# Transposing a quarter of the softmax weights by DMA in two 16-bit planes, in a decoder layer on one core

## The chip, the cores and the metric

The kernel runs on one core of one Trainium2 chip. The metric is the time of one execution on the device, in microseconds (us).

## The reference

One pre-norm decoder layer on x of shape (8, 112, 512): causal self-attention with rotary positions, cross-attention to a latent context of shape (8, 375, 128), and a gated feed-forward net in fp8. Heads: 16 of width 32.

```python
# self-attention                                     # x = x + attn(layernorm(x))
q = rope(x @ Wq + bq); k = rope(x @ Wk + bk); v = x @ Wv + bv
scores = einsum('bshd,bthd->bhst', q, k) / sqrt(32)  # causal mask
out = einsum('bhst,bthd->bshd', softmax(scores), v) @ Wo + bo
# cross-attention                                    # x = x + xattn(layernorm(x), ctx)
qp = q @ Wq.T; k, v = split(latent_kv @ Wkv_expand.T, 2)
attn = softmax(where(tril, qh @ kh.T / sqrt(32), min))  # mask: key <= query
out = (attn @ vh) @ Wout.T
# feed-forward                                       # x = x + ffn(layernorm(x))
act = gelu(qdot(x, w_gating[0])) * qdot(x, w_gating[1]); out = qdot(act, w_linear)
```

Because of the mask only the first 112 context positions take part. `qdot` casts both operands to fp8 (e4m3).

## The kernel before

**Staging.** x is held in SBUF as seven tiles of 128 tokens. Layer norm, projections and output projections go by these tiles or by column ranges; attention goes by batch (8 batches of 112 tokens). Float32 projections are done as three matmuls on a high and a low part (`mm3`, line 363; `split_evac`, lines 324 and 325, makes the two parts of an activation, `split_weight`, lines 281 and 283, those of a weight). The FFN is fp8 (lines 572 and 597).

**Attention of one batch** (`attention`, called for "a", self, and "x", cross). One step of TensorE makes the scores of all 16 heads into four banks (line 420). They form four groups of four heads, c = 0 to 3. For each group VectorE adds the mask and takes the row minimum (line 429), ScalarE takes the exponential with its row sum (line 432), VectorE the reciprocal (435), GpSimd or VectorE normalises the 112 x 448 weights P (436). TensorE transposes the group's four 112 x 112 blocks into the PSUM tile pspt (443), ScalarE or VectorE copies that to pts (`copy`, line 320). When all four groups are there, one step of 32 matmuls multiplies them by the values (AV, line 453), and its result is split into fm (`split_evac`).

**Other users of what the change touches.** `flip` (lines 332 to 335) is the DMA transpose that the kernel has already: the normalised input of the FFN, 128 x 512 in bf16 (xw), is transposed into xt on SP's queue and cast to fp8. GpSimd also does half of the weight splits (283), part of the rotary additions (402), the power of layer norm (307), the bias additions (500), and issues three casting loads of 1 MB for the FFN's weights (509, 512). SP's queue issues every other DMA: the weights' staging loads (256), the rotary row swaps (400), the values' stores (478), the outputs (605).

**Order.** All steps are put in a list when the kernel is built, and `ORDER`, a long string of step numbers, says in which order they are issued; a letter behind a number chooses the engine (a ScalarE, d VectorE, p GpSimd) where a step allows two. Each engine runs its own steps in that order and waits for the data. `CAPS` gives the number of buffers of each kind (t: temporaries of 512 floats a row, with pts, ws for weight staging and others as limits inside it); a buffer is given to the next user in the order when its last user is listed.

Of the kernel before, what the change touches and what calls it, by code (L numbers as in the profile page):

```python
# [10 lines left out]
BF = mybir.dt.bfloat16  # L11
F8 = mybir.dt.float8e4
# [19 lines left out]
PAIR = 4  # L32

# [17 lines left out]
class Plan:  # L51
# [47 lines left out]
    "p": 8, "s": 4, "t": 15, "w": 4, "w8": 1, "sm": 12, "m": 4, "pt": 1, "av": 1, "ws": 4, "pts": 7, "fg": 6, "fo":  # L99
    2, "rp": 5, "xn": 3, "f": 5, "cx": 3, "P": 4, "a8": 1, "nw": 20, "warm": 1, "vt": 2,  # L100
}
ORDER = """
1 23-24 37 40 25-26 43 46 85-87 94 22 88 0 89 95-98 2-20 90-91 21 38 103 112 39p 99 41 42p 92 100-101 44 113 104 102
114 105 45d 106 93 107 257-258 272-273 259 274 47 275-276 32 28 49 115 29 311 116 48p 277 260 278 108 50 261 279-282
262 109 263 283 320 51d 312 264-267 55 35 52 36 56 117 110 287 53 73 58 284 111 57d 64 118-119 288-290 268 120 59 54d
321 60d 74 75p 65 27 61 286 269 66d 302 322 62 63d 313 303-304 323 305 67 33 76 30 70-71 68 72p 155 291 156-157
121-122 158 123 159 292 124-129 160 130 161-163 131 189 132 190 164 191 165 293 192 294 193-194 324 134 133 1128 544
34 31 271 285 136 166-167 170 135 195 295 168 69d 196 296 197 297 138-139 198 140 199 141-142 298 200 143 172 202 299
201 144 173 145 174 146-147 175 148 545 77 169 1129 546p 314-315 306 223 176-177 149 178-180 224 240 225 547 82 325
137p 78d 151 150 153 83 316 307 171p 152 204 270 241 181-183 185 184 242 326 226-227 243 228 530 327-328 154d 528-529  # L110
203 187 186 244 229 206 230 245 231-232 246 548 233 207 247 234 248-249 236 235 250 308 208 309 209-210 317 211 318
212-215 310 188d 205p 329 216 251-253 330-333 217 334-335 219 319 218 237-238 254 79 255 220-221 336 465-469 337 470
346-347 338 348-349 339 350-352 340 353 471-472 354 473 355 474 356-357 256d 239d 341-342 222d 380 475 397 476 398 359
80 565 477 84d 358 360 592 361 343 549p 1130p 527 362p 81p 300 363-366 399 580 578 478-479 594 582 608 584 606 566 570
596 367-369 602 604 568 572 590 593 609 567 381 510 382 511 370-371 512 383 372 513-516 373-374 569 573 571 574
375-376 517-521 400 384 401 385 402 607 597 605 579 583 603 522 575d 585 581 591 595 617 576 414 386 586 587p 577a 523
377 301 344 524 378 415 387-388 588 416 403 389 610 618 598 620 622 599d 624 630 611d 634 623 589a 417 390-391 418 600
419 404 420 405-406 421 407 392 636 601d 621 635 619 625 612 422-423 408 424-425 631 626 642 632 393 646 654 637 633
643 613a 658 660 638 648 647 649 659 409-410 345p 627p 379p 639p 431 448 432 628 629a 655 614 394-395 644-645 427 426
650 656 412 428 411 429 640 449 433-434 450 435 615 531 651p 641d 657 661 690 616 721 662 693 663p 652 695 697 691 727  # L120
653a 698 480 436-438 481 439 664 482 451-454 483 455-457 440 458 441-442 484-485 459 731 729 719 709 715 733 707 703
692 665d 696 694 705 699 710 728 722 720 708 732 706 704 525 413p 700d 717-718 701 702a 716 666 763 430p 443-444 711
712p 460 667 723 462-463 550 446 445 668 724p 396p 713 730 734 714a 768 461 735 766 769 486 1139-1141 1142a 788 767
1135 725 726a 736p 1136-1137 1143 487-488 1144-1145 792 764 794 770-771 765 778 776 780 790 1138d 772 489 737 495 490
496 491 497 464p 773p 447p 779 777 738a 804 782 795 800 802 806 783 781 492 793 789 791 784 807 803 801 805 774 739
836 775d 1146d 796 853 855 851 785p 786 797p 841 787d 837 808 498 669 499-500 670 501 798 740 854 852 856 842 849
843-844 838 879 799d 877 875 839-840 880 850 526 809p 671 502 672 503-504 673-675 810 676 505 677 506 678-679 845 873
865 861 811a 846p 867 857 863 741 876 864 874 868 866 878 862 858p 847 909 812 507 848d 912 493-494 508-509 553 556
532 859 916 869 914 928 881 922 870p 917 913 860a 742-743 680 744 926 745 871 746-747 681 910 813 915 927 551 936-937
923 911 872d 934 940 814 924 682 882p 918 748-751 883 752 815 753 816-826 884a 935 925 929 533 754 946-947 941 950 930  # L130
755-756 952 938 554 948 683 827-828 919p 534p 931p 920 885 951 939 921a 886 982 932 942 829 684 887 949 953 557 985
983 830 987 933d 552p 943p 831 888-893 944 894-897 559 986 984 988-989 954 955p 990 945a 1011 1009 997 1007 991 1001
999 956 1012 685 992p 555p 1131-1133 898-899 995 998 1002 1000 996 957d 1021 1013 1025 1019 1003 1023 993 958 900 994d
1055 1004p 1005 1010 1014 1022 1008 959 1026 1024 1020 1006a 1134a 558p 541 538 535 961-967 1015 901 1016p 1070 902
1060 1056 1027 1068 1058 960 1072 1062 1057 1059 1063 1061 1017 757 1080 1018d 968-972 1028p 1029 560 1069 1086 686
1064 1094 1084 1074 1030a 1071 1151-1152 687 1031 973 1065p 1087 1073 1075 1032 1066 832 1096 1082 903 1098 1076 1081
1097 1083 1099 1085 1095 1092-1093 1067d 1033 542 688 1147 1153 1154d 1034-1038 1077p 1078 1039-1040 1088 758 904
1079d 1089p 1100 1148 833 1149 1041-1042 1090 1150d 689 1043-1044 1159 1045 536 1091a 1101p 974 905 975 759 834-835
1046 1102 1103a 1160-1161 906 1104 760 1155-1157 539 1105 1162d 761 1158a 1163 1107-1111 1106 537d 762 1047-1048 543d
907-908 540d 1164 1198 1112-1114 1211 1115 1199 1116 1212 1200 1117 1201-1203 1118 1165p 1119-1122 976 564 977-978  # L140
561d 1049-1050 1224 1204 1225 1205 1213 1226 1214-1215 1227 1216 1206 1228 1207-1208 1217 1209 1229-1230 1237-1238
1231 1218-1222 1232 1239-1246 1233 1247 1234 1248 1235 1223d 1210d 1123-1124 1249d 1051 1236a 979-981 1125 1350 1126
1379 1363 1357 1355 1052 1367 1369 1365 1351 1353 1393 1389 1387 1391 1377 1275 1250 1276 1251 1277 1252 1278-1279
1253 1280-1281 1254 1282-1283 1255-1256 1284 1257-1259 1285-1288 1260 1289-1293 1261 1294-1295 1380 1358 1053 1356
1354 1352 1054 1359 1360d 1364 1366 1390 1378 1370 1361 1262 1296 1263 1297 1381 1375 1127 1368 1371 1372d 1402 1362a
1388 1376 1382 1392 1394 1373 1407 1374a 1403 1408 1300 1264-1265 1301 1298 1383 1417 1405 1395 1384p 1266 1302 1267
1303-1304 1268 1305 1385 1306 1269 1409 1299d 1421 1431 1386d 1429 1415 1406 1404 1418 1410-1411 1396p 562 1412p
1325-1326 1270 1307 1327-1328 1271 1308 1272 1397 1309 1273 1310-1312 1329 1422 1430 1416 1398a 1419 1441 1274d 1427
1443 1420 1432 1423 1433 1444-1445 1434 1439-1440 1446 1428 1313 1330 1314 1331 1315-1316 1413 1399-1400 1442 1424p
1414d 1475 1425 1332-1337 1435 1482 1436p 1426a 1338 1317 1339 1437 1340 1318 1341-1343 1319 1344 1483 1492 1494 1476  # L150
1493 1478-1479 1495 1480 1447 1490 1401 1438d 1502 1504 1481 1477 1484 1506 1491 1448p 1345 1320 1346-1347 1449 1170
1321 1171 1348 1172 1516 1166 1322-1323 1167-1168 1450a 1518 1488 1512 1349d 1500 1514 1485p 1486 1503 1505 1489 1496
1517 1324a 1507 1173a 1451 1548 1501 1452 1497p 1487d 1169d 1508 1561 1498 1174 1454-1456 1175 1515 1499a 1453 1549
1513 1551-1552 1519 1550 1565 1567 1509p 1510 1176 1553 1575 1555 1520 1577 1511d 1177d 1576 1556 1554 1557 1563 1573
1566 1562 1521p 1568 1564 1178 1457 1179 1458 1180 1459-1461 1522 1462 1190 1463 1191 1464 1558p 1587 1579 1589 1580
1523d 1585 1569 1181d 1591 1192 1465 1559 1524 1574 1193a 1586 1590 1588 1578 1525 1592 1570p 563 1621 1466 1560d 1581
1638 1571 1622 1626 1593 1636 1624 1628 1526 1572a 1639 1637 1623 1582p 1527-1531 1583 1650 1634 1652 1584a 1629 1627
# [33 lines left out]
def kernel(  # L191
# [28 lines left out]
    def tmp(name, dt=F32, extra=()):  # L220
        return Buf(("t", *extra), lambda k: sb.tile([128, 512], dt, tag=f"t{k['t']}", name=nm(name)))
# [20 lines left out]
    for _ in range(CAPS["nw"]):  # L242
        op("pe", lambda: T.matmul(out=warm(), lhsT=zero()[:, :128], rhs=zero(), start=True, stop=True),
           r=[zero], w=[warm])
# [416 lines left out]
```

## Time and profile before

| | |
|---|---|
| median of 3 runs | 281.54 us (281.28 to 281.7) |
| the profiled execution | 281.24 us, span 279.3 us |
| TensorE busy | 273.7 us, 98% of the span |
| VectorE, ScalarE, GpSimd busy | 221.8, 194.3, 109.5 us |
| transposes of softmax weights (line 443) | 256 matmuls |
| DMA transposes (xt from xw) | 7, of 128 x 512 bf16 |

The profile is one execution taken by the hardware profiler. Busy times of an engine can lie beside those of others; the chain of work lists the steps which, each released by the one before, end with the last instruction. A row of a group reads: line, engine, operation, output<-inputs, shapes, count | busy us, mean ns of one | idle time of the engine ahead of them, and what ended it. Matmuls are pipelined, so the mean of one is longer than the pace of several.

### The profile page before, as it was taken

The page shows a single profiled execution, that of the slowest core. Times are in us where ns is not written, and L with a number is a line of the kernel's source. Part 1 is how long each engine was busy: PE and PEld are TensorE (multiplying, and loading weights), DVE is VectorE, ACT ScalarE, POOL GpSimd, SP SyncE. Part 2 cuts the span into 40 slices and gives each one's busy share as a digit, 9 for nine tenths or more (in the row PEclk, how much of TensorE's full clock was granted, in tenths as well). Part 3 has the DMA queues.
Part 4 walks back from the last instruction along what each step waited for, and adds up shares of the span by engine and source line. Part 5 has one row for each costly group of instructions (what it writes and reads, how often), then busy time and mean ns, then how long its engine had stood idle before and what let it go on. Part 6 is the DMA issues. An engine that isn't in the chain of part 4 may idle for free.

```text
span 279.3 us, 7540 instructions
## 1 busy us (share of the span) xinstructions
PE 273.7 (98%) x2648; PEld 223.6 (80%) x2648; DVE 221.8 (79%) x909; ACT 194.3 (70%) x697; POOL 109.5 (39%) x123
## 2 busy tenths in 40 slices
PE   8999999999999999999999999999999999999994
PEld 3788988898888888878999887888888887776654
DVE  3896887889988889897897889998967858565372
ACT  3854410787999999970599999999886864633141
POOL 2727680347796398614035454732201200101000
PEclk9999999999999999999999999999999999999999
DMA  7994322332030413016909609410010100001005
GB/s 229 362 339 158 137 104 87 113 129 76 17 104 26 153 40 115 2 35 43 102 9 87 69 3 105 49 38 4 2 40 2 38 2 0 20 1 41 0 38 190
DMA packets 18742, 21.70 MB, mean 78 GB/s; under 512 B 7056, under 2 KB 11536, under 8 KB 18704
## 3 DMA queue, kind: packets, MB, share of 16 engines
q1 hardware_dynamic: 15584, 18.07, 20.1%
q0 software_dynamic: 3120, 3.15, 12.7%
q8 instruction: 21, 0.34, 0.5%
q14 instruction: 17, 0.14, 0.2%
HBM read 22.39 MB, written 1.84 MB: 87 GB/s over the span
## 4 chain that ended last, share of the span: by engine, by line
PE 92%; DVE 4%; ACT 1%; DMA 1%; issue 0%; POOL 0%; POOLq 0%
PE psm L363 44%; PE psfg L572 18%; PE pspt L443 10%; PE psfo L597 9%; PE pss L420 6%; PE psav L453 5%; PE psm L349 2%; DVE fml L325 1%; DMA x_sb<-in_x_dram 1%; DVE wxqwl L283 1%; DVE v_sb L320 0%; DVE lnx L304 0%; ACT xna L311 0%; ACT wvwh L281 0%; DVE xnx L313 0%
## 5 line engine op out<-in xcount | busy, mean ns | idle before, releaser
L432 ACT ACTIVATE P<-P,at 112x112 f32<-112x112 f32 x256 | 96.5, 381 | 8.3 <-DVE at L429 8.1
L436 POOL TENSOR_TENSOR P<-P,at 112x448 f32<-112x448 f32 x52 | 48.5, 938 | 52.6 <-DVE at L435 35.8
L429 DVE CUSTOM_DVE_ANT_0 P<-pss,mask 112x112 f32<-112x112 f32 x256 | 55.7, 265 | 3.5 <-PE pss L420 2.2
L432 ACT ACTIVATION_READ_ACCUMULATOR P<-P,at 112x1 f32 x256 | 48.7, 190 | 0.0
L443 PE MATMUL pspt<-ident,P 112*112 112x112 f32 x256 | 35.9, 262 | 0.0
L443 PEld LDWEIGHTS pspt<-ident,P 112*112 112x112 f32 x256 | 27.5, 133 | 7.6 <-issue 1.2
L572 PE MATMUL psfg<-x,wgwl 128*128 128x256 fp8e4 (+1 forms) x256 | 28.5, 259 | 0.0
L572 PE MATMUL psfg<-x,wgwh 128*128 128x256 fp8e4 (+1 forms) x256 | 28.0, 259 | 0.0
L572 PEld LDWEIGHTS <-wgwl 128*128 128x128 fp8e4 x256 | 21.9, 98 | 5.0 <-issue 1.4
L572 PEld LDWEIGHTS <-wgwh 128*128 128x128 fp8e4 x256 | 22.1, 98 | 4.5 <-issue 0.9
L320 ACT CAST gf<-psfg 128x512 bf16<-128x512 f32 x34 | 18.6, 585 | 9.0 <-PE psfg L572 9.0
L320 DVE CAST gf<-psfg 128x512 bf16<-128x512 f32 x22 | 15.0, 685 | 9.3 <-PE psfg L572 9.3
L582 DVE TENSOR_TENSOR gf<-gf 128x512 bf16<-128x512 bf16 x28 | 12.4, 453 | 12.2 <-ACT gf L580 8.3
L320 ACT COPY pts<-pspt 112x448 f32<-112x448 f32 x36 | 18.9, 526 | 4.2 <-PE pspt L443 2.2
L429 DVE DVE_READ_ACCUMULATOR2_ANT at<- 112x1 f32 x256 | 21.3, 83 | 0.0
L580 ACT ACTIVATE gf<-gf 128x512 bf16<-128x512 bf16 x28 | 16.6, 631 | 5.5 <-DVE gf L320 5.4
L320 DVE COPY pts<-pspt 112x448 f32<-112x448 f32 x28 | 17.3, 617 | 2.2 <-PE pspt L443 2.0
L307 POOL TENSOR_TENSOR lnf<-lnf,mhalf 128x1 f32<-128x1 f32 x7 | 4.1, 585 | 37.0 <-DVE lnf L306 37.0
L420 PE MATMUL pss<-k,q 32*112 32x112 f32 x512 | 16.9, 268 | 0.0
L420 PEld LDWEIGHTS pss<-k,q 32*112 32x112 f32 x512 | 14.0, 172 | 3.1 <-issue 2.0
L320 ACT CAST ob<-psfo 128x512 bf16<-128x512 f32 (+1 forms) x7 | 3.5, 494 | 18.3 <-PE psfo L597 18.3
L597 PE MATMUL psfo<-wlin,a 128*128 128x512 fp8e4 x64 | 15.6, 379 | 0.0
(140 smaller groups left out, 644.4 us busy)
## 6 DMA issues: line engine op xcount, KB each, us to landing
qt<-qs SPq DMA_DIRECT2D x32, 112.0 KB, 2.0
x_sb<-in_x_dram SPq DMA_DIRECT2D x7, 256.0 KB, 4.9
out_dram<-x_sb SPq DMA_DIRECT2D x6, 256.0 KB, 2.3
wst<-in_Wv_dram SPq DMA_DIRECT2D x4, 256.0 KB, 4.9
wst<-in_Wq_dram SPq DMA_DIRECT2D x4, 256.0 KB, 5.1
wst<-in_Wo_dram SPq DMA_DIRECT2D x4, 256.0 KB, 3.7
wst<-in_Wk_dram SPq DMA_DIRECT2D x4, 256.0 KB, 5.1
wst<-in_WoutT_dram SPq DMA_DIRECT2D x4, 256.0 KB, 3.3
```

The lines of the kernel that those rows point to most:

```text
L320: lambda e: A.copy(dst(), src()) if e == "act" else V.tensor_copy(dst(), src()), r=r, w=w)
L363: T.matmul(out=out(), lhsT=l(a), rhs=r(b), start=q == 0, stop=q == 3 * tot - 1)
L420: T.matmul(out=banks[r]()[:S, j * S : (j + 1) * S], lhsT=qk[0]()[rs, c, t0 : t0 + S], rhs=qk[1]()[rs, c, t0 : t0 + S], start=True, stop=True)
L429: op("dve", lambda ps=ps, r=r, j=j, Pv=Pv, sm=sm: V.tensor_tensor_reduce(Pv()[:, r, :], ps()[:S, j * S : (j + 1) * S], mask(), -SCALE, BIG ...
L432: op("act", lambda r=r, Pv=Pv, sm=sm: A.activation(Pv()[:, r, :], Pv()[:, r, :], AF.Exp, bias=sm()[:S, r : r + 1], scale=-1.0, accum_out=s ...
L436: op(("pool", "dve"), lambda e, sm=sm, Pv=Pv: LO[e].tensor_tensor(Pv(), Pv(), sm()[:S, 8:12].unsqueeze(2).broadcast_to([S, 4, S]), ALU.mul ...
L443: T.transpose(pt()[:S, r * S : (r + 1) * S], Pv()[:, r, :], ident()[:S, :S])
L453: T.matmul(out=av()[r * 32 : (r + 1) * 32, c * S : (c + 1) * S], lhsT=v_sb()[:, b, h * 32 : (h + 1) * 32], rhs=pts()[:S, r * S : (r + 1) * ...
L572: T.matmul(out=ps()[:, j * n : (j + 1) * n], lhsT=wg()[i][:, c, (m + j) * 128 : (m + j + 1) * 128], rhs=x8()[:, c, t0:t1], start=(c == 0), ...
L580: op("act", lambda gb=gb: A.activation(gb()[:, :w], gb()[:, :w], AF.Gelu_apprx_tanh), w=[(gf, 0)])
L582: op("dve", lambda gb=gb, fb=fb: V.tensor_tensor(fb()[:, :w], gb()[:, :w], fb()[:, :w], ALU.mult), r=[(gf, 0)], w=[(gf, 1)])
L597: T.matmul(out=ps()[:, :wd], lhsT=a8()[:, m, s], rhs=wl()[0][:, m, hs], start=(m == 0), stop=(m == NH - 1))
```

## The change

Group c = 0 of each attention (four of sixteen heads, in all 16 attentions) is no longer transposed by TensorE. `flip_p` copies the low and the high 16 bits of each float32 weight into two planes of a buffer hl (1024 16-bit elements a row, each of the eight 112-wide blocks padded to 128), by GpSimd or ScalarE; one DMA transpose of 112 x 1024 puts the eight transposed blocks into xt; a copy on GpSimd or VectorE weaves the planes back into float32 pts. AV takes that pts beside the three that TensorE transposes. There are two hl buffers, whose pads GpSimd zeroes at the start, and two xt slots; t falls from 15 to 13 buffers (each now up to 1024 16-bit elements, the same bytes), ws from 4 to 3, pts from 7 to 6. `flip` lists its engines in another order. `ORDER` is a new list over 2190 steps (2172 before), engine choices included: 14 of the 16 partings and all 16 weavings are on GpSimd; 47 of the 64 normalisations are (52 before). The three casting loads of the FFN's weights are listed ahead of cross-attention's first normalisation.

```diff
+U16 = mybir.dt.uint16
+FLIP = 1
 CAPS = {
-    "p": 8, "s": 4, "t": 15, "w": 4, "w8": 1, "sm": 12, "m": 4, "pt": 1, "av": 1, "ws": 4, "pts": 7, "fg": 6, "fo":
...
+    "p": 8, "s": 4, "t": 13, "w": 4, "w8": 1, "sm": 12, "m": 4, "pt": 1, "hl": 2, "xt": 2, "av": 1, "ws": 3, "pts":
+    6, "fg": 6, "fo": 2, "rp": 5, "xn": 3, "f": 5, "cx": 3, "P": 4, "a8": 1, "nw": 20, "warm": 1, "vt": 2,
 }
 ORDER = """
...
+    hls = [act.tile([128, 1024], U16, name=f"hl{k}") for k in range(CAPS["hl"])]
+    pads = fixed(None)
+    for h in hls:
+        op("pool", lambda h=h: G.memset(h.rearrange("p (g t) -> p g t", g=8)[:, :, S:], 0), w=[pads])
...
+    LO2 = {"act": A.copy, "dve": V.tensor_copy, "pool": G.tensor_copy}
...
+    def planes(t):
+        return t.bitcast(U16).rearrange("p (n two) -> p two n", two=2)
+
+    def flip_p(P):
+        hl, xt, pts = Buf(("hl",), lambda k: hls[k["hl"]]), tmp("xt", U16, extra=("xt",)), tmp("pts", extra=("pts",))
+        halves = lambda t: planes(t()[:S, :GT]).rearrange("p two (r s) -> p two r s", r=4)
+        op(("pool", "act"), lambda e: LO2[e](
+            hl()[:S].rearrange("p (two r s) -> p two r s", two=2, r=4)[:, :, :, :S], halves(P)), r=[*((P, r) for r in range(4)), pads], w=[hl])
+        op("sp", lambda: nc.sync.dma_start_transpose(
+            xt()[:, : 8 * S].rearrange("p (g s) -> p g s", g=8), hl()[:S, :]), r=[hl], w=[xt])
+        op(("pool", "dve"), lambda e: LO2[e](
+            halves(pts), xt()[:S, : 8 * S].rearrange("p (two r s) -> p two r s", two=2, r=4)), r=[xt], w=[pts])
+        return pts
...
+                if c < FLIP:
+                    pts = flip_p(P)
+                    held.append((c, pts))
+                    continue
                 pt = bank("pt")
```

## The prediction

> **What bounds the kernel now.** I read the page's busy table and its chain of work first, to see which engine sets the time, and whether the removed steps lie on it.
>
> ```profile
> PE 273.7 (98%) x2648; PEld 223.6 (80%) x2648; DVE 221.8 (79%) x909; ACT 194.3 (70%) x697; POOL 109.5 (39%) x123
> PE 92%; DVE 4%; ACT 1%; DMA 1%; issue 0%; POOL 0%; POOLq 0%
> ```
>
> TensorE is busy for 98% of the span and 92% of the chain. The chain's split by line gives the transposes of the softmax weights (psum tile pspt, line 443) 9.5%, 26.5 us for 64 groups of four. So they are on the path, at 26.5/64 = 0.41 us a group. Next I asked for the windows of self-attention (47 to 118 us) and of cross-attention (136 to 214 us), since a mean over the kernel hides who comes second. Columns: window, its length, busy us (instructions) of PE, PEld, DVE, ACT, POOL, then clock and DMA.
>
> ```profile
> 47.00:118.00 71.00, 71.00 (x802) 59.08 (x801) 63.55 (x354) 63.90 (x288) 45.83 (x48) 1.00 0.24 76
> 136.00:214.00 78.00, 78.00 (x956) 67.09 (x960) 68.74 (x370) 72.63 (x306) 28.55 (x34) 1.00 0.39 41
> ```
>
> TensorE is full in both, at a clock of 1.00; ScalarE is close behind (93% in the second), and GpSimd has room: 25 and 49 us idle. Last, the groups by line give prices, and the rows of tile xt those of a DMA transpose that the kernel already has.
>
> ```profile
> L443 PE MATMUL pspt<-ident,P 112*112 112x112 f32 x256 | 35.9, 262 | 0.0
> L436 POOL TENSOR_TENSOR P<-P,at 112x448 f32<-112x448 f32 x52 | 48.5, 938 | 52.6 <-DVE at L435 35.8 <-DVE at L429 4.9 <-PE pspt L443 4.7
> L320 ACT COPY pts<-pspt 112x448 f32<-112x448 f32 x36 | 18.9, 526 | 4.2 <-PE pspt L443 2.2 <-issue 1.5
> L332 POOL CAST xw<-xnf 128x512 bf16<-128x512 fp8e4 x6 | 3.9, 655 | 6.1 <-issue 3.2 <-DVE xnf L313 1.6 <-PE pspt L443 1.3
> L333 SPq DMA_TRANSPOSE xt<-xw x7: 1189/1191/1311, 180.5 to 242.6; - x7
> DMA to landing us min/median/max: 2.4/2.4/2.5
> ```
>
> The 262 ns of a transpose overlap their neighbours; the chain's 0.41 us for four is the pace. The other rows are the nearest to what is added.
>
> **Removed.** One group of four transposes in each of 16 attentions: 16 x 0.41 = 6.6 us of TensorE work on the path. Bounds: a group that follows other matmuls takes 0.39 us in the chain (6.2), one that follows the scores 0.53 (8.5). I take 6.6. With them go 16 evacuations of pspt, 0.526 us on ScalarE or 0.617 on VectorE: off the path, so no gain of their own. The normalisation (0.938 us) stays.
>
> **Added, per attention.** A parting, a DMA transpose, a weaving. The two copies move 896 16-bit elements with one input. Nearest is the one-input GpSimd row above, 655 ns for 512: 0.655 x 896/512 = 1.15 us. From below: the same row unscaled, 0.65. From above: the two-input row, 0.938 x 896/448 = 1.88. I take 1.15; in the new order 14 partings and all 16 weavings go to GpSimd, two partings to ScalarE. 30 x 1.15 = 34.5 us of GpSimd beside 53.6 idle in the two windows (at 1.88 it would be 56). The transpose carries 112 x 1024 x 2 bytes, 1.75 times the row's 128 x 512 x 2: issue 2.1 us on SP and 4.2 to landing, if it grows with bytes; from below 2.4 as in the row; from above 6.3, since 256 KB weight loads landed in 3.2 us when alone and in 4.9 to 5.1 in the opening crowd (1.5 times). The crowd matters: the new order issues all three 1 MB loads of the FFN weights (13.5 to 15.4 us each, at 126, 146 and 166 us before) ahead of cross-attention's first normalisation, so the transposes of its first three batches run beside them.
>
> The Trainium skill (GPSIMD Engine Reference, "Performance versus the Vector engine" and "Engine selection") speaks against this placement: elementwise work belongs on VectorE, and the best GpSimd loop takes 1.8 cycles an element at 1.2 GHz. As an estimate from that page, 896 elements are 1.34 us, and each flipped group would be ready 0.4 us later than in my sum, some 0.6 us more over the kernel. No row here shows such a strided 16-bit copy.
>
> **Does the new path fit?** The attention-value step (AV, line 453) waits for the flipped group too, and TensorE runs in order, so all its later work waits behind. From the start of the scores to a batch's first group of transposes the lists of before hold 5.3 to 10.3 us of TensorE work, 7.2 on average, so a normalised group is there after at most 7.2. The new path then needs 1.15 + 4.2 + 1.15 + 0.2 of handover = 6.7: ready 13.9 us after the scores began, and 12.0 if the group was normalised at 5.3. Against that I add up the TensorE work that the new order puts between scores and AV, at the chain's pace (0.98 us the scores, 0.41 a group, 0.21 to 0.24 a wide matmul, 0.88 eight FFN matmuls). Self-attention, batches 0 to 7: 16.5, 16.4, 16.8, 15.2, 15.0, 13.9, 11.6, 15.6; cross-attention: 12.6, 15.0, 14.2, 14.2, 12.4, 18.4, 20.6, 25.4. Ready at 13.9 is late in three batches, by 2.3, 1.3 and 1.5 = 5.1 us; at 12.0 late in one, by 0.4. I take 2.0, nearer the low end, since in the timeline a normalisation ends some 0.7 us before its transposes begin (102.25 and 102.93).
>
> **What queues behind a wait.** The weaving waits in GpSimd's queue for its DMA. In self-attention batch 1 and cross-attention batch 2 a normalisation of the same batch stands behind it, so a late DMA also holds transposes that stayed on TensorE; elsewhere the weaving comes after the batch's last normalisation on GpSimd. On SP a flip stands ahead of values stores (line 478 before), weight loads and, in cross-attention, the xt transposes; their users come several us later, so nothing, or some tenths if a parting is late. Fewer slots (t 15 to 13, pts 7 to 6, ws 4 to 3) tie loads and temporaries closer: nothing taken, since ScalarE idled 9.3 us for Wo's loads without a stall of TensorE; at worst 0.7. The first loads and the two pad memsets move in the opening 9 us: within 0.5 either way.
>
> **The sum.** The profiled execution of before took 281.24 us (span 279.3 and 1.9 around it), 0.3 below the median 281.54. 281.24 - 6.6 + 2.0 = 276.6; with the 0.3, **276.9 us**.
>
> **Rivals.** (A) Slower: the plane copies cost as much per element as a two-input step, 1.88 us. The path is then 8.2 us; ready at 15.4, it is late in nine batches by 14.5 us together, at 13.5 in three by 3.9; the middle, 9.2, gives 281.54 - 6.6 + 9.2 = 284.1. It decides once AV waits exceed 6.6 us, 0.41 a batch. For it: strided 16-bit access has no row here, and in six batches the weaving is GpSimd's last step with under 1.9 us of TensorE work after the last transposes start. Against: other one-input copies on GpSimd are cheap. (B) ScalarE takes the gain back. In self-attention the new list gives it two partings (2.1 us at 526 ns per 448), two more fm casts (1.1), two more weight casts (1.2) and one copy less (0.5): 66.7 (busy from 44 to 121 us) + 3.9 = 70.6 us for 73.2 of TensorE work. If it gets no further than the 93% it shows in cross-attention, that takes 75.8, 2.6 more: 279.5. Against: between 99 and 107 us ScalarE was busy 8.00 of 8 us with TensorE still full. (C) All slack holds, and each removed group was worth 0.53: 281.54 - 8.5 + 0.4 = 273.4. (D) The flips arrive just late enough to cancel: within 0.2% of 281.5. That the transposes stay is excluded: the flipped group skips the pspt bank altogether.
>
> **How the numbers follow.** The forecast (275.3 to 280.0 by the bounds of its wait) has 0.46, C 0.08, B 0.18, D 0.04, A 0.24. A measurement of this kernel can tell about 0.2% (0.56 us) from no change. Faster is 0.46 + 0.08 + 0.18 = 0.72, the same 0.04, slower 0.24. The range runs from 274.3, which leaves out most of C, up to 283.6, which takes in B, D and the nearer half of A.
>
> **What would show it.** Right: pspt matmuls drop from 256 to 192, TensorE busy falls by about 6.6 us at a share of 97% or more, parting and weaving rows stand near 1.15 us, the flip lands in about 4.2, and AV waits sum to some 2 us, in self-attention batch 6 and cross-attention batches 0 and 4. A shows as AV waiting on GpSimd in nine or more batches with copies near 1.9 us; B as PE waiting on ScalarE's copies between 50 and 118 us; a landing above 6 us beside the weight loads would move the loss to cross-attention batches 0 to 3. The forecast is wrong if TensorE's busy time falls as said and the span does not follow, or if the reordered opening or the FFN tail, which I price at nothing, change by over 1 us.

## The result and the profile after

The changed kernel took 295.74 us (median of 4 runs, 295.15 to 295.93), the kernel before 281.62 beside it (4 runs, 281.28 to 282.1): a ratio of 1.0496, 95% interval 1.0474 to 1.0518. It is 14 us slower, where 4.6 us less had been forecast.

The page of the changed kernel, its busy table, the rows of the 40 slices for TensorE and its clock, and the chain:

```profile
span 294.1 us, 7499 instructions
PE 271.9 (92%) x2584; PEld 218.5 (74%) x2584; DVE 221.6 (75%) x903; ACT 191.3 (65%) x688; POOL 146.2 (50%) x156
PE   7899999999999989999930899999999999999994
PEclk9999999999999999999995599999999999999999
PE 70%; DMA 13%; DVE 11%; POOL 2%; ACT 1%; issue 1%; SPq 1%; POOLq 0%; DVEq 0%
```

The 64 transposes are gone (2584 instructions of 2648). But the busy sum of TensorE fell by 1.8 us only, the span grew by 14.8, and the chain has 13% of DMA where it had 1%. The slices show one place: in the 21st and 22nd (of 7.35 us each, from 147 us) TensorE is busy for three tenths and for nothing, and in the 22nd and 23rd the clock is at half. The chain in order of time names what stands in that hole, and the windows of that stretch (length, busy us of PE, PEld, DVE, ACT, POOL, then clock, DMA share, GB/s) show what follows.

```profile
142.37 0.93 POOL hl L420
143.33 18.27 DMA xt<-hl
161.72 1.19 POOL pts L424
162.95 1.72 PE psav L479 x32
```

```profile
148.00:153.00 5.00, 1.79 (x16) 1.58 (x14) 3.01 (x17) 2.20 (x12) 0.00 (x0) 1.00 1.11 117
153.00:158.00 5.00, 0.00 (x0) 0.00 (x0) 0.00 (x0) 0.00 (x0) 0.00 (x0) 0.70 1.07 111
158.00:163.00 5.00, 0.05 (x4) 0.05 (x8) 0.00 (x0) 0.00 (x0) 1.28 (x2) 0.50 0.32 38
163.00:166.00 3.00, 2.97 (x38) 2.42 (x38) 0.62 (x1) 1.12 (x4) 2.52 (x3) 0.50 0.00 0
166.00:169.00 3.00, 3.00 (x39) 2.71 (x39) 0.94 (x9) 1.60 (x8) 0.00 (x0) 0.55 0.42 82
169.00:172.00 3.00, 3.00 (x26) 2.96 (x25) 2.31 (x20) 3.00 (x14) 2.18 (x3) 1.00 0.00 0
```

Cross-attention's batch 0 parted its weights at 142.4, its flip (the DMA transpose of the parted weights, tile xt from hl) was issued at 143.33 and landed 18.27 us later. The attention-value step (AV) waited for it, TensorE runs in order, and from 150 to 162.9 nothing ran on it. When it went on, the clock was at 0.50, and stayed there to about 168.7: the 32 AV matmuls took 1.72 us instead of 0.9. The usual flip is quite another thing. The answer for the lines of the flip and its copies, the waits, and the DMA issues between 120 and 165 us:

```profile
L422 SPq DMA_TRANSPOSE xt<-hl x16: 1222/1236/2137, 56.1 to 226.1; - x16
DMA to landing us min/median/max: 2.9/3.0/18.3
L424 POOL COPY pts<-xt 112x896 uint16<-112x896 uint16 x16 | 19.5, 1218 | 20.4 <-DMA xt<-hl 19.8
PE psav L479 <- POOL pts L424: 13.2, 1, 13.2
```

```profile
wgwh<-in_wgat_dram POOLq DMA_DIRECT2D x1, 1024.0 KB, 13.6
wlin<-in_wlin_dram POOLq DMA_DIRECT2D x1, 1024.0 KB, 21.6
wgwl<-in_wgat_dram POOLq DMA_DIRECT2D x1, 1024.0 KB, 27.9
xt<-hl SPq DMA_TRANSPOSE x1, 18.3
```

The median flip landed in 3.0 us; one did not, and it alone made AV wait, 13.2 us in one piece. It ran while the second and third casting load of the FFN's weights, issued at 130.4 and 133.5, were still on their way, to 152.0 and 161.4. The DMA share of the windows, 1.07 to 1.11, says the same: the engines were full.

### The profile page after: what moved, and what is told of

Read it like the earlier page. It is cut to its first block, busy times and chain, and to the rows that moved or that the text cites. A ratio compares the mean times of both kernels' runs of the same rounds, so it can differ in the third digit from the quotient of the medians.

```text
span 294.1 us, 7499 instructions
## 1 busy us (share of the span) xinstructions
PE 271.9 (92%) x2584; PEld 218.5 (74%) x2584; DVE 221.6 (75%) x903; ACT 191.3 (65%) x688; POOL 146.2 (50%) x156
## 2 busy tenths in 40 slices
DMA packets 33590, 25.36 MB, mean 86 GB/s; under 512 B 21904, under 2 KB 26384, under 8 KB 33552
## 4 chain that ended last, share of the span: by engine, by line
PE 70%; DMA 13%; DVE 11%; POOL 2%; ACT 1%; issue 1%; SPq 1%; POOLq 0%; DVEq 0%
PE psm L369 33%; PE psfg L598 16%; DMA xt<-hl 9%; PE psfo L623 7%; PE pspt L469 4%; DVE P L451 4%; PE psav L479 4%; PE pss L442 3%; DMA x_sb<-in_x_dram 2%; PE psm L355 2%; DVE P L458 1%; POOL pts L424 1%; DMA wst<-in_WoutT_dram 1%; DVE fml L331 1%; SPq L261 1%
## 5 line engine op out<-in xcount | busy, mean ns | idle before, releaser
L458 POOL TENSOR_TENSOR P<-P,at 112x448 f32<-112x448 f32 x47 | 45.7, 978 | 31.7 <-DVE at L457 29.1
L424 POOL COPY pts<-xt 112x896 uint16<-112x896 uint16 x16 | 19.5, 1218 | 20.4 <-DMA xt<-hl 19.8
L479 PE MATMUL psav<-pts,v_sb 112*32 112x112 f32 x512 | 16.5, 270 | 14.1 <-POOL pts L424 13.2
L469 PE MATMUL pspt<-ident,P 112*112 112x112 f32 x192 | 28.0, 269 | 0.9 <-POOL P L458 0.4
L479 PEld LDWEIGHTS psav<-pts,v_sb 112*32 112x32 f32 x512 | 12.3, 113 | 19.4 <-POOL pts L424 13.8
L469 PEld LDWEIGHTS pspt<-ident,P 112*112 112x112 f32 x192 | 20.3, 136 | 7.7 <-POOL P L458 2.9
L326 ACT CAST gf<-psfg 128x512 bf16<-128x512 f32 x28 | 15.6, 582 | 12.7 <-PE psfg L598 12.1
L326 DVE CAST gf<-psfg 128x512 bf16<-128x512 f32 x28 | 18.4, 682 | 6.3 <-PE psfg L598 6.3
L331 DVE TENSOR_TENSOR fml<-psav,fmh 128x448 fp32r<-128x448 f32 x16 | 9.8, 614 | 13.9 <-ACT fmh L330 13.8
L330 ACT CAST fmh<-psav 128x448 fp32r<-128x448 f32 x16 | 8.4, 523 | 17.5 <-PE psav L479 17.3
```

Of the source, the lines that this page charges most:

```text
L326: lambda e: A.copy(dst(), src()) if e == "act" else V.tensor_copy(dst(), src()), r=r, w=w)
L331: op("dve", lambda: V.tensor_tensor(dst(1), src(), dst(0).bitcast(F32), ALU.subtract), r=[*rd, *keys(0)], w=keys(1))
L424: op(("pool", "dve"), lambda e: LO2[e](halves(pts), xt()[:S, : 8 * S].rearrange("p (two r s) -> p two r s", two=2, r=4)), r=[xt], w=[pts])
L458: op(("pool", "dve"), lambda e, sm=sm, Pv=Pv: LO[e].tensor_tensor(Pv(), Pv(), sm()[:S, 8:12].unsqueeze(2).broadcast_to([S, 4, S]), ALU.mul ...
L469: T.transpose(pt()[:S, r * S : (r + 1) * S], Pv()[:, r, :], ident()[:S, :S])
L479: T.matmul(out=av()[r * 32 : (r + 1) * 32, c * S : (c + 1) * S], lhsT=v_sb()[:, b, h * 32 : (h + 1) * 32], rhs=pts()[:S, r * S : (r + 1) * ...
```

## The experiments

**What each theory said.** *Collision*: the late flip shared the 16 DMA engines with the casting loads; take either away and the loss is gone. Under it two forms: *turns* (the flip's packets alternate with those of the loads, so its delay follows its own size) and *drain* (it waits until the loads are through). *Order*: the new list of steps is bad by itself. And on the missing gain: is a group worth the 0.41 us that I read from the chain, or does something else bind once TensorE is relieved?

| run | median us | ratio to before, 95% interval |
|---|---|---|
| a1_no_dma | 278.26 | 0.9876 [0.9851, 0.9902] |
| a2_bunch | 281.48 | 0.9989 [0.9977, 1.0002] |
| a3_dup | 298.52 | 1.0597 [1.0558, 1.0636] |
| a4_x0_pe | 285.76 | 1.0145 [1.0097, 1.0193] |
| b1_half | 289.92 | 1.0298 [1.0267, 1.0329] |
| b3_moved | 294.52 | 1.0473 [1.0433, 1.0513] |
| b4_split | 285.94 | 1.0148 [1.0110, 1.0186] |
| c2_idle | 294.41 | 1.0440 [1.0393, 1.0487] |
| c3_x01_pe | 280.09 | 0.9932 [0.9905, 0.9958] |
| e3_x01_again (the same kernel) | 280.37 | 0.9946 [0.9930, 0.9963] |
| c4_self_only | 287.69 | 1.0194 [1.0146, 1.0241] |
| b2_notr | 279.77 | 0.9934 [0.9916, 0.9953] |
| c1_pool_copy | 279.14 | 0.9884 [0.9849, 0.9919] |
| d2_notr_exp | 278.78 | 0.9901 [0.9880, 0.9923] |
| d3_exp | 281.46 | 0.9996 [0.9983, 1.0010] |
| e1_av3 | 287.23 | 1.0191 [1.0164, 1.0218] |
| e2_all | 277.34 | 0.9845 [0.9827, 0.9863] |

The kernel before stood at 281.46 to 282.06 beside them; where two runs are compared below, it is by their ratios.

### Is it the flips, the loads, or the order?

**a1_no_dma**: the change without its DMA transposes.

```diff
-        op("sp", lambda: nc.sync.dma_start_transpose(xt()..., hl()[:S, :]), r=[hl], w=[xt])
+        op("sp", lambda: None)
...
-            halves(pts), xt()...
+            halves(pts), hl()[:S]...[:, :, :, :S]
```

> The changed kernel without its 16 DMA transposes: the weaving reads the parted planes directly, so these four heads' weights enter AV untransposed; partings, weavings and the order stay. Theory 'collision' (one transpose beside the casting loads of the FFN weights cost 14 us of TensorE idle and some 3 us of lowered clock): 276 to 279 us. Rival 'the new order and the GpSimd copies are too slow in themselves': above 287 us, with TensorE waiting for weavings in many batches.

Measured: 278.26 us. Partings, weavings, the new order and the bunched loads are all in it, and it is 3.5 us *faster* than before. So *order* falls as the cause of the loss, and the sixteen transposes cost 1.0496 - 0.9876 of 281.6, 17.5 us, though fifteen of them land as they should.

**a2_bunch**: the kernel before with its three casting loads issued one behind the other (two tokens of `ORDER` moved).

> The kernel before, with its three casting loads listed one after another ahead of cross-attention, as the change has them; nothing else moves. If bunched loads harm only through a transpose beside them: 281.6 us within 0.6, as before. Rival 'the bunched loads slow the engines by their own traffic': 283 us or more.

Measured: 281.48, no difference. The three loads landed 13.2, 22.6 and 31.2 us after their issue (27.9 at most in the change), and no step waited for that. The loss needs both: the loads and a short transfer beside them that somebody waits for.

**a3_dup**: the change with a fourth 1 MB casting load behind the gating loads (the FFN's output weights, read into a tile that is free then).

```diff
+        if i == 1:
+            G.dma_start(out=a8(), in_=wlin.rearrange("(c p) n -> p c n", p=128))
```

> The changed kernel with a fourth 1 MB casting load (into the buffer a8, which is free until the FFN) issued right after the three. Theory 'turns' (the transpose's packets alternate with those of the loads, 58 on each DMA engine, so its delay is set by its own packets): cross-attention batch 0's transpose lands after 16 to 20 us as now, total 294 to 298 us. Theory 'drain' (it lands only when the casting loads queued ahead have drained): it lands after some 30 us, total 306 to 311 us.

Measured: 298.52. The added load and the sixteen flips of this run:

```profile
a<-in_wlin_dram POOLq DMA_DIRECT2D x1, 1024.0 KB, 38.4
DMA to landing us min/median/max: 2.9/3.0/18.9
```

With loads running to 172.0 us instead of 161.4, batch 0's flip still took 18.91 us and landed at 161.5, more than 10 us before the loads were through. *Drain* falls, *turns* holds. The total is above what I gave, because batch 1's flip now met the loads as well (issued at 165.4, 7.3 us).

**b1_half**: the change with only one of the two planes transposed; the weaving uses it twice, so the weights of that group are wrong in their low halves and the time is that of half the bytes.

```diff
-            xt()[:, : 8 * S].rearrange("p (g s) -> p g s", g=8), hl()[:S, :])
+            xt()[:, : 4 * S].rearrange("p (g s) -> p g s", g=4), hl()[:S, 512:])
```

> The changed kernel with transposes of half the size: only the plane of the high 16 bits goes through the DMA, and the weaving writes it into both halves of each weight, so those four heads' weights are rounded and repeated; order, loads and copies stay. Theory 'turns' (own packets times the load's turn): beside the loads the transpose of cross-attention batch 0 lands after 8.5 to 11 us in place of 18.3, TensorE idles 5 to 7 us there, total 283 to 288 us. Rival 'a fixed hold until a load ends': 14 us or more, total above 292 us.

```profile
DMA to landing us min/median/max: 2.4/2.5/12.6
PE psav L479 <- POOL pts L424: 7.5, 1, 7.5
```

Measured: 289.92 us. Half the size lands in 2.5 us instead of 3.0 when alone, but in 12.6 instead of 18.3 beside the loads. Landing and time are above what I gave for *turns* and below the rival's. The packet counts make the landing readable: 33590 in the change and 18741 in a1_no_dma are 928 for each flip, 58 for each of the 16 DMA engines; here it is 480, or 30. So 28 packets less were 5.7 us less, 0.20 us each. The two queues of the changed kernel between 151 and 158 us (packets, MB, share of 16 engines' time; q0 has GpSimd's loads, q1 the flip) show what a packet waits for:

```profile
q0 software_dynamic: 339, 0.69, 97.5%
q1 hardware_dynamic: 334, 0.09, 9.2%
```

Load and flip move one packet each in turn. 334 turns on 16 engines in 7 us are 0.34 us a turn, nearly all of it the load's packet, of 2 KB here. From 147.2 to 149 the load's packets are shorter (250 for 0.16 MB), 197 of the flip's get through, and a turn is 0.15 us; so the 0.20 is a mean over both and no constant. Some of the delay does not shrink with the flip's size: in the change the first packet of batch 0's flip moves 3.8 us after its issue (in b1_half, a3_dup and a4_x0_pe too), that of batch 1's, with no load under way, 1.2 us after. Why is open.

The Trainium skill (DMA: Bandwidth & Descriptors, "SWDGE vs HWDGE vs iDMA") says that transfers issued by GpSimd and by SP feed different queues inside the same DMA engines, which take them in turn. The one-for-one counts agree with that. The same page's "Rules for kernel authors" says that a transpose next to ordinary DMAs needs nothing; that line stands beside a warning of wrong data, and 3.0 us becoming 18.3 is what it does not tell.

**a4_x0_pe**, then **c3_x01_pe**: cross-attention's batch 0, then batches 0 and 1, have their first group back on TensorE; all else as in the change, with the transposes and copies put into `ORDER` by hand.

```diff
-                if c < FLIP:
+                if c < FLIP and not (kind == "x" and b < 2):     # a4_x0_pe: b == 0
```

> The changed kernel with cross-attention batch 0's first group back on TensorE. Theory 'collision': the next transpose, batch 1's, meets the end of the same loads, so its AV waits 2 to 6 us in place of the 14: 281 to 285 us. Rival 'something special to batch 0': no wait is left, 278 to 279 us.

Measured: 285.76, a little above what I gave. In the profiled execution (284.57 us) batch 0's wait is gone and the clock stays at 1.00, but now batch 1's flip, issued at 150.86, met the end of the loads and took 8.7 us:

```profile
DMA to landing us min/median/max: 2.9/3.0/8.7
PE psav L481 <- POOL pts L424: 3.1, 1, 3.1
```

> The change, with the first group of cross-attention batches 0 and 1 transposed by TensorE again; the other fourteen groups are flipped as in the change, the loads stay. Theory 'only the flips that meet the casting loads cost': every flip lands in under 4 us, no wait of the attention-value step for GpSimd above 1 us, clock 1.00 throughout, 280.5 to 283. Rival 'the order of steps in the change is bad by itself': above 284.5.

Measured: 280.09, and 280.37 when repeated. No flip takes over 4.5 us any more, and AV waits for GpSimd once, for 0.4 us:

```profile
PE 270.7 (97%) x2592; PEld 217.6 (78%) x2592; DVE 221.3 (80%) x905; ACT 190.9 (69%) x688; POOL 142.4 (51%) x152
DMA to landing us min/median/max: 2.9/3.0/4.5
```

This is a little better than I had expected, and it is the version that beats both kernels: two groups of sixteen given back, 15.5 to 15.9 us gained over the change and 1.5 to 1.9 us over the kernel before.

> The version with the first groups of cross-attention batches 0 and 1 on TensorE, once more with more rounds, as it was the only one below the kernel before that computes everything: 279.5 to 280.8 if its 0.7% is real; above 281 if the chip of that call made it.

**c4_self_only**: the same for all eight batches of cross-attention; flips in self-attention alone.

> The change with flips in self-attention alone, where no casting load runs: all eight first groups of cross-attention are on TensorE again. Theory 'only the flips that meet the loads cost, and a flip elsewhere is worth 0.2 us': 280 to 283, the same as the run with two batches put back or up to 1.5 above it. Rival 'flips that do not collide cost as well': below that run by over 1 us.

Measured: 287.69, over 4 us above what I gave. All eight flips landed within 4.6 us. TensorE was busy for 36.96 of the 40 us between 160 and 200 us, against 39.55 in c3_x01_pe, so the lost time came with the six further groups that I put back by hand, in a stretch without flips. It tells nothing about flips, only that these six steps did not go into the list without planning it anew.

### Can the loads be moved out of the way?

**b3_moved**: the gating loads 4 us earlier, the output weights' load after batch 6's weaving (three tokens moved).

> The changed kernel with only its three casting loads moved: both gating loads some 4 us earlier, behind self-attention's last normalisation but one on GpSimd's queue, wlin's behind the weaving of cross-attention batch 6, where 14 us pass without a transpose. Theory 'collision': batch 0's transpose meets the last 4 to 6 us of the gating loads, TensorE idles 0 to 3 us, 278.5 to 281.5 us. Rival (the order's other waits are the loss): above 287 us.

Measured: 294.52, no better than the change. The flips were all right (6.8 us at most), but the loads met two other transfers of SP's queue. From the chain in order of time:

```profile
123.74 15.93 DMA cst<-in_ctxT_dram
211.10 11.15 DMA xt<-xw
```

The first is a plain load of 224 KB (2.7 us in the change), the second the DMA transpose that the kernel had before (2.4). TensorE stood still behind both, for 4.3 and 6.9 us. So it is not the new transpose alone that is slow: a plain load and the old transpose on SP's queue are slowed beside a casting load too, and cost where somebody waits for them.

**b4_split**: the second gating load and the output weights' load cut into 256 KB pieces, issued between the batches' weavings.

```diff
+    def wg1(c):
+        G.dma_start(out=wg()[1][:, c : c + 1, :], in_=wgat[1][c * 128 : (c + 1) * 128, :]...)
+    def wl4(c):
+        G.dma_start(out=wl()[0][:, 4 * c : 4 * c + 4, :], in_=wlin[c * 512 : (c + 1) * 512, :]...)
```

> The changed kernel with the second gating load and wlin's load split into four pieces of 256 KB each, every piece issued after a weaving of cross-attention (batches 0 to 3, and 4, 5, 6, 6), so that a transpose meets 256 KB at the most. Theory 'turns': landings of 3 to 6 us, no idle over 2 us, 278 to 281 us. Rival 'any load beside a transpose costs it the load's whole length and more': 283 us or more.

```profile
DMA to landing us min/median/max: 2.9/3.4/5.4
```

Measured: 285.94. The hole is gone (clock 1.00 everywhere), but cross-attention's first five flips now take 3.8 to 5.4 us, and GpSimd waits for flips seven times, 10.5 us in all. TensorE in turn waits 4.0 us for normalisations, which share GpSimd's queue with the weavings (0.4 in the change). Better than the change by 10 us, worse than before, and above what I expected: many small delays instead of one large one.

### Idle time and the clock

**c2_idle**: a1_no_dma, in which GpSimd makes batch 0's weaving thirteen times, so TensorE waits as long as in the change with no flip on the DMA engines.

```diff
-        op(("pool", "dve"), lambda e: LO2[e](halves(pts), hl()...), r=[hl], w=[pts])
+        op(("pool", "dve"), lambda e: [LO2[e](halves(pts), hl()...) for _ in range(n)], r=[hl], w=[pts])
```

> The run without any transposing DMA (278.3 us; part of the computation is left out), in which GpSimd makes the weaving of cross-attention batch 0 thirteen times in a row instead of once: 12 x 1.2 = 14.4 us in which TensorE waits as long as it did for the late transpose, but with nothing added on the DMA engines. Theory 'an idle TensorE of that length is given half clock afterwards': clock about 0.5 for some 6 us behind it, and 294.5 to 297 us, all that the change costs. Rival 'the clock fell because of the DMA traffic': clock stays 1.00, 291 to 293.

```profile
155.00:160.00 5.00, 0.00 (x0) 0.00 (x0) 0.00 (x0) 0.00 (x0) 4.75 (x5) 0.50 0.43 43
163.00:166.00 3.00, 2.96 (x42) 2.34 (x38) 0.62 (x1) 1.40 (x5) 2.24 (x3) 0.50 0.00 0
166.00:169.00 3.00, 3.00 (x39) 2.76 (x40) 1.31 (x14) 1.60 (x8) 0.03 (x1) 0.50 0.02 5
169.00:172.00 3.00, 3.00 (x25) 2.95 (x25) 1.92 (x16) 3.00 (x15) 2.15 (x3) 0.99 0.00 0
```

Measured: 294.41 us, 15.9 above a1_no_dma, and the clock is at half while the DMA engines rest (share 0.00 and 0.02 from 163 to 169 us). So a waiting TensorE alone brings the half clock (n is 13 for batch 0 and 1 elsewhere; that is the whole difference from a1_no_dma). The price can be read from TensorE's busy sum: 271.9 us both here and in the change, 269.1 in a1_no_dma with the same 2584 instructions, 2.8 us more. The clock alone gives much the same: half of the 5.7 us that TensorE worked at half clock in the change is 2.9. The sum itself varies by up to 0.9 us between two executions of one kernel (270.7 in c3_x01_pe, 271.6 in e3_x01_again). The wait (13.2 us in the change) and these 2.8 are 16 of the 17.5 us.

How long a wait it takes can be read from windows of 1 us. The clock fell 2.8 us after the last matmul in b1_half, 2.9 in c2_idle, 4.2 in a3_dup, 5.2 in the change, 4.4 and 3.5 at the two waits of b3_moved. It came back 3.5 and 3.4 us after work went on in b3_moved (the first from 140.9 to 144.4), 4.0 in a3_dup, 5.5 in b1_half (156.85 to 162.3), 5.7 in the change and 6.4 in c2_idle. In a4_x0_pe TensorE stood still for 3.1 us (157.8 to 160.9) and the clock stayed at 1.00 in the execution that was profiled; two of the other three took 287.12 and 286.78 us at a mean clock of 0.985 and 0.986, so there it did fall, after waits whose length was not profiled. The six stretches at half clock lasted 3.41, 6.83, 10.24, 13.65 (twice) and 17.07 us, one to five times 3.41: the clock changes in steps of that length. The Trainium skill (TensorE: Matmul & The Clock Gate, "What's actually happening") gives one window of some 3.4 us for both ways, running freely, so that the moment varies. The lengths agree with it. Whether a wait of some 3 us brings the half clock may then depend on where in the steps it falls; no run here shows that.

### Why the relief was worth so little

**b2_notr**: the kernel *before*, old order, in which TensorE no longer transposes the first groups; their copies take the untransposed weights (this part of the result is left out).

```diff
-                op("pe", tr, ...)
+                op("pe", tr if c else (lambda: None), ...)
...
+                    copy(lambda pts=pts: pts()[:S, :GT], lambda P=P: P()[:S, :GT], GT, [P, pt], [pts])   # c == 0
```

> The kernel before, old order, without the TensorE transposes of each attention's first group (the copy takes P itself, so these four heads' weights enter AV untransposed). It prices the removal alone. By the prediction's 0.41 us a group: 275.1 us (274 to 276). Rival 'the freed time was partly cover for other engines': 277 to 279 us.

Measured: 279.77. The same 64 matmuls that the change removes, and nothing else: 1.9 us (0.66% of 281.6), not 6.6, and less than the rival gave too.

**c1_pool_copy, d2_notr_exp, d3_exp, e2_all** relieve other engines. c1 makes b2's copies on GpSimd. d2 is b2 without three of four exponentials of each first group; d3 is the kernel before without these; e2 is d2 with three of four masking steps and the normalisation of those groups left out too. In d2, d3 and e2 the mask's value is a small constant, so that weights without their exponential stay finite.

```diff
-                    op("act", lambda ...: A.activation(Pv()[:, r, :], ...
+                    op("act", lambda ...: c == 0 and r > 0 or A.activation(Pv()[:, r, :], ...        # d2, d3, e2
-                    op("dve", lambda ...: V.tensor_tensor_reduce(
+                    op("dve", lambda ...: c == 0 and r > 0 or V.tensor_tensor_reduce(                # e2
-                op(("pool", "dve"), lambda e, ...: LO[e].tensor_tensor(Pv(), Pv(), ...
+                op(("pool", "dve"), lambda e, ...: c == 0 or LO[e].tensor_tensor(Pv(), Pv(), ...     # e2
```

> The kernel before without the transposes of each batch's first group on TensorE (that group's weights are copied untransposed, so part of the computation is left out), as in the run that came to 279.8 us; now these 16 copies (7 on ScalarE at 0.53 us, 9 on VectorE at 0.62) are made by GpSimd. Theory 'ScalarE is the bound that took the place of TensorE in the attention stages': 3.7 us less on ScalarE and 5.5 less on VectorE there, so the time falls to 277.0 to 278.7. Rival 'the written order is the bound, whoever copies': 279.2 to 280.5.

Measured: 279.14, 3.3 us below the kernel before beside it; the interval reaches that of b2_notr. The median lies between what the two theories gave, so by itself it settles nothing.

> The kernel before without the first groups' transposes (279.8 us as a run of its own), and with three of the four exponentials of each first group left out too (the weights of that group are not the reference's): 16 x 3 x 0.58 = 28 us less on ScalarE. Theory 'ScalarE holds back what TensorE gives': the freed TensorE work now comes through, 274.5 to 277.5. Rival 'the written order or a group's real worth of 0.1 us': 278.8 to 280.

> The kernel before with its transposes, and the same 28 us of ScalarE work left out. Theory 'TensorE is the bound as long as its transposes are there': 280.3 to 281.6, at most 0.4% off. Rival 'ScalarE held the kernel before back as well': below 280.

> The run without the first groups' transposes and with three of four of their exponentials left out (278.8 us), and now three of four of their masking steps on VectorE (48 x 0.35 = 17 us) and their normalisation on GpSimd (15 us) left out too. Theory 'VectorE, ScalarE and GpSimd together stand close behind TensorE in the attention stages': the freed TensorE work comes through, 275 to 277.3. Rival 'something else holds the 4 us back, whatever these engines do': 278 to 279.5.

Measured: d3 281.46, no difference; d2 278.78, 2.8 us below before; e2 277.34, 4.4 below. With its transposes, the kernel does not care how fast ScalarE is. Without them, ScalarE's relief brings 0.9 us, which is not clear of noise (the intervals of b2_notr and d2_notr_exp overlap), and the relief of VectorE and GpSimd together another 1.6, which is; the runs do not tell these two apart. So d2 ends at the edge of its rival's range: ScalarE alone does not hold the time back. The busy sums of TensorE:

```profile
PE 269.6 (97%) x2584; PEld 216.9 (78%) x2584; DVE 222.7 (80%) x909; ACT 193.6 (70%) x697; POOL 109.8 (40%) x123
PE 269.4 (98%) x2584; PEld 217.0 (79%) x2584; DVE 208.9 (76%) x808; ACT 177.9 (65%) x601; POOL 99.3 (36%) x112
```

b2_notr first, then e2_all. The four runs of the old order without the groups have 269.1 to 269.9 us, four with them 273.7 to 274.5 (before, a2_bunch, d1_twice, d3_exp). The means lie 4.7 us apart: that is what the 16 groups were worth, 0.29 us each, and e2_all turns nearly all of it into time (4.4 us).

**e1_av3** adds work instead: the attention-value step sums the first group's product three times (so these heads come out too large).

```diff
-                for r in range(4):
+                n = 1 if c else 3
+                for t, r in ((t, r) for t in range(n) for r in range(4)):
...
-                             rhs=pts()[:S, r * S : (r + 1) * S], start=True, stop=True)
+                             rhs=pts()[:S, r * S : (r + 1) * S], start=t == 0, stop=t == n - 1)
```

> The kernel before, in which the attention-value step adds up the product of each batch's first group three times (so those four heads come out three times too large): 16 x 16 = 256 more matmuls of the form that ran 32 to 0.88 to 0.97 us, 7.0 to 7.8 us more on TensorE and nothing on other engines. Theory 'TensorE sets the time of the kernel before': 288.5 to 289.5. Rival 'its 98% hide slack': below 286.

```profile
PE 280.2 (98%) x2904; PEld 229.8 (80%) x2904; DVE 223.0 (78%) x909; ACT 195.2 (68%) x697; POOL 109.7 (38%) x123
```

Measured: 287.23, 5.4 us more (1.91%), between what the theory and the rival gave. TensorE's busy sum grew by 5.7 to 6.5, so most of what is added shows: it is the bound upwards. The price per matmul was lower than I gave (48 in 1.36 us against 32 in 0.97).

**d1_twice** was meant to do this with the transposes themselves, made twice.

> The kernel before with the four transposes of each batch's first group made twice: 16 more groups on TensorE. If a group is worth the 0.41 us that the chain showed and TensorE alone is the bound: 281.5 + 6.6 = 288 (287 to 289). If a group is worth what TensorE's busy sum lost without them (4.1/16 = 0.26 us): 285 to 286.5. If there is slack behind TensorE: below 284.

Measured: 281.89, ratio 1.0001 (0.9988 to 1.0015), but the program that ran had 2648 TensorE instructions, as before: writing the same tile twice had been reduced to once. It says nothing about the question.

**And the new order?** In a1_no_dma, two windows late in self-attention show the same thing from the other side:

```profile
100.00:110.00 10.00, 8.82 (x107) 6.29 (x100) 10.00 (x52) 9.18 (x40) 6.59 (x8) 1.00 0.02 7
110.00:120.00 10.00, 9.57 (x80) 7.39 (x80) 9.41 (x50) 9.49 (x40) 7.54 (x10) 1.00 0.26 81
```

VectorE is busy for all ten us of the first, TensorE for 8.82. Before, TensorE had 10.00 in both. Of the 1.6 us that TensorE idles here, 1.2 end with VectorE and 0.4 with GpSimd. The last self-attention batch's AV comes at 124.1 us, 3 us later than before (121.1), though eight groups had left TensorE by then. From 47 us on it had idled those 1.6 us and worked 75.5 us against 74.1, since the new order also puts other work before that AV.

## Why the prediction was wrong, step by step

- **The price of a flip beside the loads: the step that failed.** I had seen that the first three cross-attention batches would flip beside the loads, and bounded that by "from above 6.3, since 256 KB weight loads landed in 3.2 us when alone and in 4.9 to 5.1 in the opening crowd". It was 18.27. The sum put 4.2 us on each landing and 2.0 on all waits for flips together; one wait alone was 13.2. The row was the wrong neighbour: those loads shared the engines with others of SP's queue, not with a 1 MB casting load of GpSimd's, and the factor of a 256 KB load did not carry over to 58 small packets an engine that each wait for a load's packet. a1_no_dma (without flips), a2_bunch (loads alone), a3_dup (longer loads) and b1_half (smaller flip, and the packet counts) show the mechanism; c3_x01_pe shows that it is the whole loss. The remark under "what would show it" named the place, but had neither a price nor a chance in the range. It was also one batch, not three: batch 0 held TensorE until the loads were through, so batch 1 came after them.
- **The clock was no term of the sum.** Every wait was counted at its length. A wait of 13 us cost some 2.8 more in slow matmuls (c2_idle).
- **6.6 us of TensorE work was 4.7.** The chain put 0.41 us on a group of four; the busy sums with and without the groups lie 4.7 us apart, 0.29 a group. So 0.12 us of what the chain gives a group stays when the group goes; why, no run shows. The bounds that I gave (6.2 to 8.5) were the spread of the same wrong reading.
- **"TensorE is full in both" was read as "alone".** Of the 4.7 us, 1.9 came through in the old order and 3.5 in the new one, since the other engines stood right behind: with VectorE, ScalarE and GpSimd relieved, 4.4 came through (e2_all). Rival B had ScalarE doing that; it was right in kind, but ScalarE's part, 0.9 us, is the smaller and not clear of noise.
- **What was right.** The copies: 1.15 taken, 0.93 for the parting and 1.22 for the weaving measured, so rival A (1.88) is out; the skill's estimate of 1.34 was above both. The usual landing was 3.0 against 4.2, with an issue of 1.24 against 2.1. Fifteen of the sixteen batches had their flipped group in time: in c3_x01_pe AV waits 0.4 us for GpSimd in all, so the 2.0 us taken for lateness were too many. The opening moved by 0.6 us (self-attention's first AV at 64.9 against 64.3).
- **Two slips that decided nothing.** GpSimd's idle time in the two windows is 74.6 us by the rows shown (25.2 and 49.4), not 53.6. In rival B, 77.0 us less eight groups at 0.41 are 73.7 us of TensorE work, not 73.2.

Added up from the runs: 3.5 us gained by all of the change but its DMA (a1_no_dma), 13.2 lost to the wait, 2.8 to the clock, and 1.5 left for the other fifteen flips and the rest: 14.0.

## What to carry to other kernels

Before a wait is put on a DMA, look at which other transfers are under way then, on any queue: here a small transfer with many packets paid for a large load's packet at each turn, so its price in the crowd followed its own packet count and the size of the load's packets, not its time when alone. Price a long wait of TensorE with half clock for the work behind it: in the profiled executions all six waits of 4.3 us or more brought it, for 3.4 to 6.4 us of work, and a4_x0_pe, with a wait of 3.1 us in the execution profiled, had it in two of its four. And a step's share of the chain is not what removing it brings: take the engine's busy sum with and without, over several executions, and ask which engine is next. One engine at 98% does not say that the others have room in the same stage: in self-attention VectorE and ScalarE were both at 90%.

## What the runs showed that I had not expected

- Casting loads of 1 MB from GpSimd's queue made short transfers of SP's queue 4 to 6 times slower: flip 3.0 to 18.3 us, half flip 2.5 to 12.6, plain load of 224 KB 2.7 to 15.9, the 128 x 512 transpose 2.4 to 11.2 (the second of two at once; the first took 8.9). Packets of both queues went one for one, and the smaller transfer paid. The loads were held up less: the second and third landed 21.6 and 27.9 us after their issue with a flip beside them, 18.6 and 26.0 without (a1_no_dma).
- After a wait of 4.3 us or more TensorE ran at half clock for its next 3.4 to 6.4 us, and each stretch at half clock was a whole multiple of 3.41 us. After one of 3.1 us it did not, in the one execution that was profiled.
- Added TensorE work showed by 5.4 of some 6 us, removed work by 1.9 of 4.7, in the same kernel with the same list of steps.
